# Two more chunks of ten get their layer-1 bias from GpSimd and ScalarE, not from a TensorE product

## The chip, the core and the metric

The kernel runs on one core of a Trainium2 chip. The time is device microseconds of one execution; 9 runs of the kernel before have a median of 577.31 us (576.45 to 579.66).

## What is computed

A graph layer over 128 graphs of 64 nodes with 128 channels. For each pair (i, j) of nodes in a graph a small network makes a message; the messages over the edges of the adjacency matrix are summed at i, and a second network of the same form updates the node:

```python
pair_feats = concatenate([f_i, f_j], axis=-1)            # 256 channels
h = layernorm(relu(pair_feats @ w0 + b0), g0, be0)       # layer 0
h = layernorm(relu(h @ w1 + b1), g1, be1)                # layer 1
messages = (h @ w2 + b2) * adj[..., None]
agg = messages.sum(axis=2)
out = x + mlp_upd(concatenate([x, agg], axis=-1))
```

All of it is float32.

## The kernel before

**Tiles and chunks.** The kernel computes messages for edges only. Two graphs make a pair; each graph of a pair has 640 edge places, which are filled by one-hot selection matrices (`S`, made of comparisons, with halves that are moved there by DMA). 128 edge places are a tile, four tiles a chunk (512 columns): 160 chunks in all. Five chunks are a quad (four graphs of edges), ten chunks a block (eight graphs, which share input loads and one update of 512 nodes).

**A chunk's path.** `layer0(n)` selects the two nodes' layer-0 rows with the S matrices (L539, TensorE) and ScalarE applies relu with the bias into `h` (L542). `stats0(n)` turns the four tiles (L548) and VectorE takes mean and variance of each edge (L552, `bn_stats`). The first layer norm is not applied to `h`: its scale is kept as one standard deviation per edge, and layer 1 is computed as relu(h w1c + std0 b1b), where `w1c` has the norm folded in. Since relu keeps a positive scale, the scale drops out in the second layer norm. `layer1(n)` computes h w1c into a PSUM bank `z` (L609, eight matmul records a chunk, two passes of each float32 product) and ScalarE applies the relu (L612) to give `y`; `stats1(n)` takes the statistics of `y` (L619). `reduce` sums `y` over the edges of each node, weighted by the inverse second deviation (L695).

**The bias std0 times b1b in the bank.** It is added in one of two ways:
- by TensorE: an extra product (L606) of the turned, split standard deviations `sdT` with a table `b1t`, 80 rows by 512 columns, ahead of the four products of the chunk;
- by a seed: ScalarE writes std0 times b1b into the bank beforehand (L597, four instructions of 128 columns, each scaled by one column of the standard deviations), and the products add to it.

From chunk 2 to chunk 151, those whose number ends in 0, 1, 2, 6, 7 or 9 are seeded, two iterations before their layer 1; all others have the TensorE product.

**The standard deviations.** Once per quad: when the fifth chunk's `stats0` is done, GpSimd computes m from the statistics (`square_sum`, L249 to L253), ScalarE takes the root m_sd (L259) and rounds it (`sh`, L566), GpSimd makes the rest of the split (L567), TensorE turns it (L572) and ScalarE copies it out (`sdT`, L577). A second such chain after layer 1 gives `m_sq` (L273, ScalarE) and its inverse `m_q` (L278, VectorE), from which GpSimd makes the weights `w` (L682).

**The order.** Nothing is scheduled automatically: `edge_path` records every engine's instructions in the order of the program. The main loop runs over iterations n; in each of them chunk n is in layer 0 and chunk n - 8 in layer 1 (`L1` = 8). Everything else is put into a plan by `at(n, place, function)`: it says in which iteration, and at which place in it, a function is called. The places come in the order a, m, [layer1], b, [layer0, stats0], k, [stats1], x, x1, x2, e0, e1, e. Each engine runs its instructions in that order, and waits where one needs something that is not there yet. In the timeline at 268 to 275 us iterations 79 to 82 are seen: the y at 268.24 is that of chunk 71, at 270.51 of chunk 72, at 272.63 of chunk 73.

**What else stands near the change.** In iterations that end in 9, 0 and 1: `distance` (d, L482, ScalarE), the update's `usdb` (L777, ScalarE), its turn `uh` (L740, TensorE), its copy `uhT` (L745, ScalarE) and its second layer (L754, TensorE), `residual` (xo, L734, GpSimd), `node_rows` (the cast i, L497, GpSimd). The layer-0 PSUM bank is a single one, so `layer0` of the next chunk waits for `h` of the one before; the layer-1 banks are two, used in turn.

**Inputs.** Blocks 0 and 1 have their adjacency and node features in buffers of their own (`an0`, `xn0`); those of later blocks rotate over three and five buffers and are loaded by SyncE's DMA queue, `load_adj` 25 iterations before the block. `odd_weights` checks that the adjacency is 0 or 1.

Of the kernel before, what the change touches and what calls it, by code (L numbers as in the profile page):

```python
# [9 lines left out]
F32 = mybir.dt.float32  # L10
# [4 lines left out]
ALU = mybir.AluOpType  # L15
# [8 lines left out]
def tile_gnn(  # L24
# [40 lines left out]
    nc = tc.nc  # L65
    B, N, C = x.shape
    P = 128
# [6 lines left out]
    CH = 4  # L74
    QC = QT // CH
    NCHK = NQ * QC
    PB = 4
    NB = NP // PB
    CPB = NCHK // NB

    xf = x.rearrange("b n c -> (b n) c")
    of = out.rearrange("b n c -> (b n) c")
    adjp = adj.rearrange("(p g) i j -> (g i) p j", g=2)

    const = ctx.enter_context(tc.tile_pool(name="const", bufs=1))
# [10 lines left out]
    def col(ap, name, eng=nc.sync):  # L96
        return load(ap.rearrange("(c o) -> c o", o=1), [P, 1], name, eng)
# [2 lines left out]
        return load(ap.rearrange("(o c) -> o c", o=1), [1, C], name, eng)  # L100


    an0 = const.tile([P, 2, PB, N], F32, name="an0")
    xn0 = const.tile([P, 2, PB, C], F32, name="xn0")

    def load_first(b, q0, q1):
        nc.sync.dma_start(xn0[:, b, q0:q1], xf[(b * PB + q0) * P:(b * PB + q1) * P, :]
                          .rearrange("(q p) c -> p q c", p=P))

    nc.sync.dma_start(an0[:, 0], adjp[:, 0:PB, :])  # L110
    load_first(0, 0, 2)
    w0a = mat(mw0[0:C, :], "w0a", nc.scalar)
    w0b = mat(mw0[C:2 * C, :], "w0b", nc.scalar)
    load_first(0, 2, PB)
    b0c = col(mb0, "b0c")
    nc.sync.dma_start(an0[:, 1], adjp[:, PB:2 * PB, :])
    load_first(1, 0, PB)
    w1 = mat(mw1, "w1")
    g0c = col(mg0, "g0c")
# [48 lines left out]
    W = {}  # L168
# [66 lines left out]
    def bc(t, n, axis=1):  # L235

        s = [P, n, C] if axis == 1 else [P, C, n]
        return t.unsqueeze(axis).to_broadcast(s)
# [48 lines left out]


    def edge_path(es):
        blkp = es.enter_context(tc.tile_pool(name="blk", bufs=3))  # L290
        adp = es.enter_context(tc.tile_pool(name="adp", bufs=2))
        tpp = es.enter_context(tc.tile_pool(name="tpp", bufs=8))
        sp = es.enter_context(tc.tile_pool(name="sp", bufs=4))
# [1 line left out]
        yp = es.enter_context(tc.tile_pool(name="yp", bufs=12))  # L295
        lp = es.enter_context(tc.tile_pool(name="lp", bufs=3))
        wp = es.enter_context(tc.tile_pool(name="wp", bufs=2))
        updp = es.enter_context(tc.tile_pool(name="upd", bufs=1))
        stp = es.enter_context(tc.tile_pool(name="stp", bufs=5))
        ps_k = es.enter_context(tc.tile_pool(name="ps_k", bufs=1, space=PSUM))  # L300
# [21 lines left out]
        def zbank(k):  # L322
            return ps_z[k].tile([P, CH * C], F32, name=f"z{k}")
# [4 lines left out]
        def at(n, place, fn, *args):  # L328
            plan.setdefault((n, place), []).append((fn, args))
# [3 lines left out]
                fn(*args)  # L333

        blocks = {b: {} for b in range(NB)}
        TP, S, H, ST0, V0, SD, SH, Y, ST1, Q, OH, WT, YS, MK, D, IR, JR, SR, Z = ({} for _ in range(19))


        def load_adj(b):
            if b < 2:  # L340
                blocks[b]["an"] = an0[:, b]
                return
            an = blkp.tile([P, PB, N], F32, name="an", bufs=3)
            nc.sync.dma_start(an, adjp[:, b * PB:(b + 1) * PB, :])
            blocks[b]["an"] = an

        def load_x(b):
            if b < 2:
                blocks[b]["xn"] = xn0[:, b]
                return  # L350
            xn = blkp.tile([P, PB, C], F32, name="xn", bufs=5)
            nc.sync.dma_start(xn, xf[b * PB * P:(b + 1) * PB * P, :]
                              .rearrange("(q p) c -> p q c", p=P))
            blocks[b]["xn"] = xn
# [225 lines left out]
        SEEDED = set()  # L580

        def z_of(n):

            if n not in Z:
                Z[n] = zbank(n % 2).rearrange("p (t c) -> p t c", t=CH)
            return Z[n]

        def seed(n):
# [6 lines left out]
            for t in range(CH):  # L595
                k = CH * c + t
                nc.scalar.activation(Z[n][:, t, :], W["b1b"], AF.Copy, scale=SR[q][:, k:k + 1])  # L597

        def layer1(n):

            q, c = divmod(n, QC)
            ps = z_of(n)
            del Z[n]
            h = H.pop(n)
            if n not in SEEDED:
                nc.tensor.matmul(ps, lhsT=SD[q], rhs=W["b1t"][:, CH * c:CH * c + CH, :],  # L606
                                 start=True, stop=False, skip_group_check=True)
            for t in range(CH):
                nc.tensor.matmul(ps[:, t, :], lhsT=h[:, t * P:(t + 1) * P], rhs=W["w1c"],  # L609
                                 start=False, stop=True, skip_group_check=True)  # L610
            Y[n] = yp.tile([P, CH, C], F32, name="y")
            nc.scalar.activation(Y[n], ps, AF.Relu)  # L612
# [190 lines left out]
        L1 = QC + 3  # L803
# [8 lines left out]
        for b in range(NB):  # L812
            o = b * CPB
            if b > 1:
                at(max(o - 25, 0), "a", load_adj, b)
                at(max(o - 12, 0), "a", load_x, b)
            if b > 0:
                r = max(o - 12, 1)
                at(max(o - 14, 0), "m", rank, b)
                at(r, "x", count, b)  # L820
                at(r + 1, "a", count_out, b)
                at(r + 1, "a", degrees, b)
                at(max(o - 9, r + 1), "e", place, b)
                at(max(o - 7, r + 3), "e", place_out, b)
                at(max(o - 7, 13), "m", odd_weights, b)
                at(o - 3, "x", turn_x, b)
                at(o - 2, "a", turn_x_out, b)
            for half, n in ((0, o - 2), (1, o + 3)):
                if n >= 0:
                    at(n, "x2", rows, b, half)  # L830
                    at(n + 1, "a", rows_hi, b, half)
                    at(n + 1, "m", rows_lo, b, half)
        for b in reversed(range(NB)):
            o = b * CPB
            n = o + QC + SC
# [35 lines left out]
        for p in range(NP):  # L871
            n = p * TG * 2 // CH
# [13 lines left out]
            q, h = divmod(p, 2)  # L886
# [4 lines left out]
        for q in range(NQ):  # L891
            n = q * QC + QC if q else LEAD
# [12 lines left out]
        for n in range(2, NCHK - L1):  # L905
            if n % CPB in (0, 1, 2, 6, 7, 9):
                at(n + L1 - 2, "x", seed, n)

        warm = ubank()
        for n in range(7):
            nc.tensor.matmul(warm[:, 0:P], lhsT=mean_m, rhs=mean_m, start=True, stop=True)
        load_adj(0)
        load_x(0)
        load_adj(1)
        load_x(1)
        rank(0)
        count(0)
# [54 lines left out]
        stats0(0)  # L974
        at(0, "x", turn_x, 0, 2, PB)
        at(1, "a", lambda: turn_x_out_rest())
        at(18, "m", odd_weights, 0)

        def turn_x_out_rest():
            nc.scalar.copy(blocks[0]["xnT"][:, 2 * P:PB * P], blocks[0].pop("x_ps")[:, 2 * P:])  # L980
# [46 lines left out]
        for n in range(last + 1):  # L1027
            run(n, "a")
            run(n, "m")
            if n == NCHK:  # L1030
                stats0(n - 1)
            if 0 <= n - L1 < NCHK:
                layer1(n - L1)
            run(n, "b")
            if n + LEAD < QC or QC <= n < NCHK:
                layer0(n if n >= QC else n + LEAD)
            if n + 1 < QC or QC <= n - 1 < NCHK - 1:
                stats0(n - 1 if n > QC else n + 1)
            run(n, "k")
            if 0 <= n - L1 < NCHK:  # L1040
                stats1(n - L1)
            for k in ("x", "x1", "x2", "e0", "e1", "e"):
                run(n, k)
# [3 lines left out]
    with ExitStack() as es:  # L1047
        es.enter_context(tc.manual_schedule())
        flag = edge_path(es)
# [160 lines left out]
```

## Time and profile before

| | |
|---|---|
| median of 9 runs | 577.31 us (576.45 to 579.66) |
| the profiled execution | 576.57 us, span 574.8 us |
| mean granted TensorE clock | 0.986 |
| ScalarE seeds L597 | 360, 133.6 us, 371 ns each |
| TensorE bias products L606 | 70, 33.8 us, 483 ns each |

Engines are PE (TensorE), PEld (its weight loads), DVE (VectorE), ACT (ScalarE), POOL (GpSimd) and SP (SyncE, which issues DMA). A line of the timeline gives the start in us from the start of the span, the length in us, the engine, the line of the kernel, the operation, what it writes and reads, and its size; in brackets stands the idle time of the engine before it and what ended it. Instructions of one engine overlap at their ends: the time that one costs is seen from its start to the next one's start.

### The profile page before, as it was taken

The numbers are of one execution on the slowest core, as the hardware profiler recorded it, in microseconds if no ns is written. First come the engines' busy times: TensorE is split into PE (matmuls) and PEld (weight loads), VectorE is DVE, ScalarE is ACT, GpSimd is POOL, SyncE is SP. The second block draws the span as 40 slices with busy tenths as digits, with TensorE's granted clock in tenths as the row PEclk, the third lists the DMA queues.
The fourth block names the chain that finished last, engine by engine and source line by source line (L and its number), as shares of the span: only waits on it lengthen the run. The fifth ranks groups of instructions, "written<-read, shape, count | busy, mean of one in ns | idle before, by whom it ended". The sixth has DMA issues, their size and how long they took to land. (4 is left out here: it accounts for less than half of the span.)

```text
span 574.8 us, 15748 instructions
## 1 busy us (share of the span) xinstructions
PE 548.9 (95%) x5303; PEld 514.9 (90%) x5303; DVE 479.8 (83%) x1944; ACT 476.7 (83%) x1149; POOL 339.4 (59%) x898
## 2 busy tenths in 40 slices
PE   6798999999999999999999999999999999998894
PEld 4597889999999999999999999999999999988883
DVE  5678789797989889798989989798988979896686
ACT  6677979898888989898888989888898989886434
POOL 3344465675757666565767657575766656556342
PEclk8889999999999999999999999999999999999999
DMA  4464535365564655458453554555465464631201
GB/s 101 102 146 107 127 93 143 93 118 127 125 135 107 140 108 130 106 108 153 113 141 83 140 114 116 127 125 134 99 136 120 121 106 99 135 93 31 35 21 40
DMA packets 90769, 63.21 MB, mean 110 GB/s; under 512 B 57398, under 2 KB 74812, under 8 KB 90684
## 3 DMA queue, kind: packets, MB, share of 16 engines
q1 hardware_dynamic: 90396, 62.03, 48.9%
q8 instruction: 43, 0.70, 0.5%
q14 instruction: 42, 0.34, 0.2%
q10 hardware_dynamic: 288, 0.13, 0.1%
HBM read 6.82 MB, written 4.19 MB: 19 GB/s over the span
## 5 line engine op out<-in xcount | busy, mean ns | idle before, releaser
L552 DVE BATCH_NORM_STATS2 st<-hT 128x6 f32<-128x128 f32 x640 | 142.2, 286 | 36.6 <-PE hT L548 35.2
L609 PE MATMUL z<-w1c,h 128*128 128x128 f32 x1280 | 172.2, 277 | 0.0
L609 PEld LDWEIGHTS z<-w1c,h 128*128 128x128 f32 x1280 | 161.1, 192 | 8.2 <-issue 5.1
L597 ACT ACTIVATE z<-b1b,m_sd 128x128 f32<-128x128 f32 x360 | 133.6, 371 | 8.7
L619 DVE BATCH_NORM_STATS2 st<-y 128x6 f32<-128x128 f32 x640 | 138.1, 281 | 2.7 <-ACT y L612 1.4
L612 ACT ACTIVATE y<-z 128x512 f32<-128x512 f32 x160 | 94.5, 591 | 26.6 <-PE z L609 24.9
L542 ACT ACTIVATE h<-hps,b0c 128x512 f32<-128x512 f32 x160 | 109.4, 684 | 4.0 <-PE hps L539 3.9
L548 PE MATMUL hT<-ident,h 128*128 128x128 f32 x640 | 98.2, 276 | 1.6 <-DVE st L552 1.5
L682 POOL TENSOR_TENSOR w<-oh,m_q 128x320 f32<-128x320 f16 x126 | 91.8, 741 | 9.9 <-PE hT L548 5.3
L539 PE MATMUL hps<-s,abl 128*128 128x512 f32 (+3 forms) x256 | 93.5, 377 | 1.7 <-DVE abl L473 0.9
L548 PEld LDWEIGHTS hT<-ident,h 128*128 128x128 f32 x640 | 76.9, 142 | 11.9 <-ACT h L542 1.3
L497 POOL CAST i<-tp 128x640 fp32r<-128x640 f16 x58 | 41.6, 718 | 66.6 <-DVE tp L488 48.7
L539 PE MATMUL hps<-s,abh 128*128 128x512 f32 (+3 forms) x256 | 79.7, 330 | 0.0
L695 PE MATMUL ys<-y,w 128*64 128x128 f32 x1280 | 76.9, 275 | 0.0
L695 PEld LDWEIGHTS ys<-y,w 128*64 128x64 f32 x1280 | 69.2, 137 | 4.2 <-issue 3.6
L249 POOL TENSOR_TENSOR m_d<-st 128x20 f32<-128x20 f32 x62 | 16.3, 263 | 91.0 <-DVE st L552 78.0
L521 DVE TENSOR_TENSOR j<-mk,cmpt 128x320 fp32r<-128x320 f32 x124 | 59.1, 476 | 3.0 <-PE mk L513 3.0
L539 PEld LDWEIGHTS hps<-s,abl 128*128 128x128 f32 x256 | 50.3, 196 | 3.6 <-ACT h L542 2.1
L482 ACT ACTIVATE d<-slot,mid 128x640 f16<-128x640 f16 x64 | 52.7, 824 | 0.0
L539 PEld LDWEIGHTS hps<-s,abh 128*128 128x128 f32 x256 | 50.5, 197 | 0.0
L473 DVE TENSOR_TENSOR abl<-mu,abh 128x512 fp32r<-128x512 f32 (+1 forms) x33 | 22.3, 675 | 31.2 <-ACT abh L467 31.1
L513 PE MATMUL mk<-tp,posall 128*128 128x320 f16 x126 | 38.2, 303 | 3.5 <-POOL posall L397 2.5
(224 smaller groups left out, 978.0 us busy)
## 6 DMA issues: line engine op xcount, KB each, us to landing
s<-i SPq DMA_DIRECT2D x124, 160.0 KB, 2.7
s<-j SPq DMA_DIRECT2D x124, 160.0 KB, 2.6
xn<-in_x_dram SPq DMA_DIRECT2D x15, 256.0 KB, 3.7
out_dram<-uo SPq DMA_DIRECT2D x15, 256.0 KB, 2.4
an<-in_adj_dram SPq DMA_DIRECT2D x16, 128.0 KB, 2.6
oh<-tp SPq DMA_TRANSPOSE x64, 3.4
xn<-in_x_dram SPq DMA_DIRECT2D x2, 128.0 KB
out_dram<-uo SPq DMA_DIRECT2D x2, 128.0 KB, 2.6
```

Source lines behind the costliest of these rows:

```text
L482: nc.scalar.activation(D[p], slot, AF.Abs, bias=blocks[b]["mid"][:, q:q + 1], scale=-1.0)
L521: nc.vector.tensor_tensor(JR[p][:, c], MK.pop((p, k))[:, 0:HC], cmpt[:, c], op=ALU.is_equal)
L539: nc.tensor.matmul(ps[:, c:c + w], lhsT=ab[:, g % 4, :], rhs=s, start=(k == 0), stop=(k == 1))
L542: nc.scalar.activation(H[n], ps, AF.Relu, bias=b0c)
L548: nc.tensor.transpose(ps[:, t, :], H[n][:, t * P:(t + 1) * P], ident)
L552: nc.vector.bn_stats(ST0[q][:, CH * c + t, :], ps[:, t, :])
L597: nc.scalar.activation(Z[n][:, t, :], W["b1b"], AF.Copy, scale=SR[q][:, k:k + 1])
L609: nc.tensor.matmul(ps[:, t, :], lhsT=h[:, t * P:(t + 1) * P], rhs=W["w1c"], start=False, stop=True, skip_group_check=True)
L612: nc.scalar.activation(Y[n], ps, AF.Relu)
L619: nc.vector.bn_stats(ST1[q][:, CH * c + t, :], Y[n][:, t, :])
L682: (nc.vector if p == NP - 2 else nc.gpsimd).tensor_tensor(WT[p][:, :, g, :], OH[p][:, :, g * N:(g + 1) * N], Q[q][:, k:k + TG].unsqueeze(2 ...
L695: nc.tensor.matmul(YS[b][g * N:(g + 1) * N, k, :], lhsT=w[:, t, g, :], rhs=y, start=(t == 0), stop=(t == TG - 1))
```

## The change

Chunks whose number ends in 3 or 4, from chunk 3 to 144, are no longer biased by TensorE: these are 30 chunks. In iteration n + 5 of chunk n, at its last place, GpSimd multiplies b1b by the chunk's four standard deviations, 128 by 512, into a new tile `sb` (two buffers). In iteration n + 6, place x, ScalarE copies it into the bank. The 30 L606 go; chunks that end in 5 or 8 keep theirs, so that the turn of the standard deviations stays.

The buffers of blocks 0 and 1 become the first of the rotating ones, so the separate 6 KB per partition go. For that `load_adj` comes 19 and not 25 iterations before its block, and `odd_weights` of block 0 is called in iteration 9 and not 18. In the built program the DVE order differs only in that last step; SyncE has its loads in the new places; no other instruction changes its place.

```diff
-    an0 = const.tile([P, 2, PB, N], F32, name="an0")
-    xn0 = const.tile([P, 2, PB, C], F32, name="xn0")
+    blkp = ctx.enter_context(tc.tile_pool(name="blk", bufs=3))
+    an0 = [blkp.tile([P, PB, N], F32, name="an", bufs=3) for b in range(2)]
+    xn0 = [blkp.tile([P, PB, C], F32, name="xn", bufs=5) for b in range(2)]
...
+        sbp = es.enter_context(tc.tile_pool(name="sbp", bufs=2))
...
+        def products(n):
+
+            q, c = divmod(n, QC)
+            SB[n] = sbp.tile([P, CH, C], F32, name="sb")
+            nc.gpsimd.tensor_tensor(SB[n], bc(W["b1b"], CH), SR[q][:, CH * c:CH * c + CH]
+                                    .unsqueeze(2).to_broadcast([P, CH, C]), op=ALU.mult)
+
+        def seed_from(n):
+            z_of(n)
+            SEEDED.add(n)
+            nc.scalar.copy(Z[n], SB.pop(n))
...
-                at(max(o - 25, 0), "a", load_adj, b)
+                at(max(o - 19, 0), "a", load_adj, b)
...
             if n % CPB in (0, 1, 2, 6, 7, 9):
                 at(n + L1 - 2, "x", seed, n)
+            elif n % CPB in (3, 4):
+                at(n + L1 - 3, "e", products, n)
+                at(n + L1 - 2, "x", seed_from, n)
...
-        at(18, "m", odd_weights, 0)
+        at(9, "m", odd_weights, 0)
```

More of the change, by code (lines that the diff above doesn't have):

```diff
@@ L100, in row @@
         return load(ap.rearrange("(o c) -> o c", o=1), [1, C], name, eng)
-    an0 = const.tile([P, 2, PB, N], F32, name="an0")
-    xn0 = const.tile([P, 2, PB, C], F32, name="xn0")
+    blkp = ctx.enter_context(tc.tile_pool(name="blk", bufs=3))
+    an0 = [blkp.tile([P, PB, N], F32, name="an", bufs=3) for b in range(2)]
+    xn0 = [blkp.tile([P, PB, C], F32, name="xn", bufs=5) for b in range(2)]
     def load_first(b, q0, q1):
-        nc.sync.dma_start(xn0[:, b, q0:q1], xf[(b * PB + q0) * P:(b * PB + q1) * P, :]
+        nc.sync.dma_start(xn0[b][:, q0:q1], xf[(b * PB + q0) * P:(b * PB + q1) * P, :]
                           .rearrange("(q p) c -> p q c", p=P))
-    nc.sync.dma_start(an0[:, 0], adjp[:, 0:PB, :])
+    nc.sync.dma_start(an0[0], adjp[:, 0:PB, :])
     load_first(0, 0, 2)
@@ L115, in tile_gnn @@
     b0c = col(mb0, "b0c")
-    nc.sync.dma_start(an0[:, 1], adjp[:, PB:2 * PB, :])
+    nc.sync.dma_start(an0[1], adjp[:, PB:2 * PB, :])
     load_first(1, 0, PB)
@@ L289, in edge_path @@
     def edge_path(es):
-        blkp = es.enter_context(tc.tile_pool(name="blk", bufs=3))
         adp = es.enter_context(tc.tile_pool(name="adp", bufs=2))
@@ L335, in edge_path @@
         blocks = {b: {} for b in range(NB)}
-        TP, S, H, ST0, V0, SD, SH, Y, ST1, Q, OH, WT, YS, MK, D, IR, JR, SR, Z = ({} for _ in range(19))
+        TP, S, H, ST0, V0, SD, SH, Y, ST1, Q, OH, WT, YS, MK, D, IR, JR, SR, Z, SB = ({} for _ in range(20))
         def load_adj(b):
             if b < 2:
-                blocks[b]["an"] = an0[:, b]
+                blocks[b]["an"] = an0[b]
                 return
@@ L348, in load_x @@
             if b < 2:
-                blocks[b]["xn"] = xn0[:, b]
+                blocks[b]["xn"] = xn0[b]
                 return
```

## The prediction

> **What bounds the kernel now.** I read the page's totals first, then the busy time of one stretch of the steady part, then the timeline of each engine inside it.
>
> ```profile
> PE 548.9 (95%) x5303; PEld 514.9 (90%) x5303; DVE 479.8 (83%) x1944; ACT 476.7 (83%) x1149; POOL 339.4 (59%) x898
> ```
> ```profile
> 263.00:296.00 33.00, 33.00 (x332) 31.55 (x331) 29.11 (x120) 29.48 (x72) 21.31 (x57) 1.00 0.59 122
> ```
> The second line (us, then PE, PEld, DVE, ACT, POOL busy, granted clock) says that TensorE has no idle time there. The first y relu (L612) of a block stands at 263.44 and that of the next block at 296.28: 32.85 us for ten chunks, within 0.03 in all blocks from 100 to 490 us. So a matmul that goes is time won, unless TensorE then has to wait. Whether it has to is seen at the place of the two removed matmuls, where the ScalarE queue runs like this (start, length, what; in brackets idle time before):
>
> ```profile
> 269.59 0.83 ACT L482 ACTIVATE d<-slot,mid 128x640 f16<-128x640 f16 x1
> 270.31 0.30 ACT L273 ACTIVATE m_sq<-m_v,eps_c 128x20 f32<-128x20 f32 x1
> 270.51 0.59 ACT L612 ACTIVATE y<-z 128x512 f32<-128x512 f32 x1
> 270.99 0.69 ACT L542 ACTIVATE h<-hps,b0c 128x512 f32<-128x512 f32 x1
> 271.56 0.41 ACT L777 ACTIVATE usdb<-bu1b,um_sd 128x128 f32<-128x128 f32 x1
> 271.85 0.59 ACT L745 COPY uhT<-ma 128x512 f32<-128x512 f32 x1
> 272.63 0.60 ACT L612 ACTIVATE y<-z 128x512 f32<-128x512 f32 x1 [0.19 <-PE z L609]
> 273.40 0.31 ACT L259 ACTIVATE m_sd<-m,eps_c 128x20 f32<-128x20 f32 x1 [0.17 <-POOL m L253]
> 273.75 0.22 ACT L566 CAST sh<-m_sd 128x40 fp32r<-128x40 f32 x1
> ```
> ScalarE has 83% over the span, but here it runs from 268.24 to 273.40 with 0.36 us of rest, all of it after 272.44. On TensorE and its weight loads:
>
> ```profile
> 270.87 0.60 PE L740 MATMUL ma<-ident,uh 128*128 128x128 f32 x4
> 271.23 0.47 PE L606 MATMUL z<-b1t,sdT 80*128 80x512 f32 x1
> 271.54 1.05 PE L609 MATMUL z<-w1c,h 128*128 128x128 f32 x8
> 274.51 0.48 PE L606 MATMUL z<-b1t,sdT 80*128 80x512 f32 x1
> 274.82 0.27 PE L609 MATMUL z<-w1c,h 128*128 128x128 f32 x1
> ```
> ```profile
> 274.37 0.12 PEld L572 LDWEIGHTS ma<-ident,sh 128*80 128x80 f32 x1
> ```
> Between the two removed L606 stands L572, the turn of the split standard deviations. It needs sh from GpSimd:
>
> ```profile
> 272.97 0.40 POOL L253 TENSOR_TENSOR m<-m_d,m_s 128x20 f32<-128x20 f32 x1
> 274.05 0.27 POOL L567 TENSOR_TENSOR sh<-m_sd,sh 128x40 fp32r<-128x40 f32 x1
> ```
> sh ends at 274.32 and L572's weights start at 274.37. Where TensorE demonstrably waits for sh, they start 0.05 us after its end too:
>
> ```profile
> PEld ma L572 <- POOL sh L567: 4.0, 3, 1.5
> ```
> So this chain (statistics of chunk 79 on VectorE, five GpSimd steps, root m_sd and split on ScalarE, sh on GpSimd, L572) has no slack at all, though no idle time shows it. It is the point on which the change turns.
>
> **The change part by part.** *Removed: 30 L606.* A row says 0.47 us, but matmuls overlap, so the price is what it adds between its neighbours. L740 to L609 takes 0.67 us with L606 (270.87 to 271.54) and 0.44 without (284.21 to 284.65); L572 to L609 takes 0.34 with (274.48 to 274.82) and 0.11 without (291.07 to 291.18). That is 0.23 us each, 6.9 us in all if nothing waits.
>
> *Added: 30 GpSimd products* (512 columns, two inputs). The nearest rows are xo L734, 1.28 us, and the bias table L659 on 80 partitions, 1.13 us. Two per block stand around xo at 264.03; with them GpSimd is done by about 267.7. Its next step starts at 268.83 after 3.53 us of idle time, so the products hide in that gap, and ScalarE needs the first at 269.6. Queued behind them are xo (nine iterations before its use), the cast i (which waits for VectorE until 268.83 anyway) and nothing else. If that cover were gone, each us late would be a us of ScalarE wait per block. The Trainium skill (GPSIMD Engine Reference, Engine selection) speaks against this step: a two-input elementwise operation is about twice as slow there as on VectorE. By that rule the step is badly placed; by the idle row it costs nothing, and the sum uses the row.
>
> *Added: 30 ScalarE copies* of 512 columns from SBUF to PSUM, which the trace does not have. What counts is the time c from its start to the next instruction's. Lower bound: the same copy from PSUM, L745 or L612, 0.48. Upper bound: the cast of 640 columns from SBUF, L495, 0.63 (31.73 to 32.37). Columns cost 0.84 ns (d L482 at 0.72 for 640 against usdb L777 at 0.29 for 128), so 128 columns off the cast leave c = 0.52, which I take. The Trainium skill (ScalarE: Activation LUTs, Step-by-step) says that writing PSUM is faster than writing SBUF; the seeds L597 are indeed shorter than usdb (371 against 396 ns), but their start-to-next is 0.31 against 0.29, so I give no discount. With 25 ns off, the sum below would come out 0.4 to 0.6 us lower.
>
> *Where the copies stand.* By the built order the first stands between usdb and d (269.59), the second between usdb and uhT (271.85). What is queued behind them moves:
> 1. The first moves m_sq by c. VectorE's L278 waits for m_sq (it starts 0.03 after it, as at 286.39) and had 0.07 us to spare at 270.72; so it and the statistics behind it move by c - 0.07 = 0.45, and m on GpSimd and m_sd with them.
> 2. Both move uhT, y and m_sd in ScalarE's own order: y then starts at 272.33 + 2c, m_sd at 272.81 + 2c, that is 2c - 0.59 = 0.45 later than before.
> 3. By either way sh and L572 are 0.45 us late: weights at 274.82. After such a wait the next matmul follows 0.145 us later (62.30 to 62.45 behind L572), so L609 starts at 274.96, where before it started at 274.82, 0.45 behind the same weights: **0.14 us later**, where the two removed matmuls alone would have made it 0.46 earlier. On the way TensorE also waits about 0.15 for h (end 272.20) at the next L539; that wait lies inside the later one.
> 4. After that ScalarE has a rest of 0.63 us before the next y, so the lateness is TensorE's alone and the next block starts with the old phase.
>
> The tight place occurs in 13 blocks (L572 at 110, 143, ... 504 us): 13 x 0.14 = +1.8 us. In the first two blocks TensorE already waits over 1 us at L572 (45.89, 78.44), so the first removed matmul gains nothing; the second gains 0.23 in each, less 0.16 in the second block, where m_sq had 0.36 to spare before VectorE asks for it: -0.3 us. Sum: **+1.5 us** on the profiled execution, 576.57 to 578.1. That execution lies 0.74 below the median, so the predicted median is 577.31 + 1.5 = 578.8.
>
> *Moved at no cost.* The sharing of buffers issues the same loads. The adjacency load goes six iterations later, ahead of the s<-i transfers: its issue of 0.59 us falls into SyncE's wait for the cast i (277.37), it lands 2.6 us later and is read five iterations (16 us) later; if late, rank and the statistics behind it would wait. odd_weights(0) goes from iteration 18 to 9: two VectorE steps of 0.41 and 0.42 us in a stretch where VectorE has 26.4 us of 33; from -0.8 to +0.8 us if that cover fails, and I take 0.
>
> **The rivals.**
> *Faster: the chain does not move.* The mechanism: TensorE keeps what it saves. For it speaks that TensorE is full and ScalarE only 89% busy in the stretch. If the copies cost the chain nothing, L572 still waits for sh at 274.37 and only the second removal counts: 15 x 0.23 to 0.31 = -3.5 to -4.7, 572.6 to 573.8; if the chain came earlier too, -6.9, 570.4. The point of decision is c: below 0.38, where c - 0.07 is less than the 0.45 - 0.145 = 0.31 that L606's absence saves behind L572, the block gets shorter. Against it: 128 columns alone take 0.31.
> *Slower by more: c is at its upper bound.* With c = 0.63 the queue moves m_sd by 0.67, a block loses 0.36, 13 x 0.36 - 0.3 = +4.4, 581.7.
> *GpSimd late:* products behind a wait for statistics. 2 us of margin at 269.6 speak against it; each us beyond is +13, so 590 and up.
> *No net change:* gain and loss meet, as at c = 0.48 (0.41 - 0.31 = +0.10 per block, +1.0, 578.3); that is the lower end of my own forecast.
>
> **How the numbers follow.** A measurement here tells 0.2%, 1.2 us, from no change. My forecast has 0.68, and its own range is c from 0.48 to 0.60: 578.3 to 580.9; about two fifths of it lie within 0.2%. The faster rival has 0.15, the dear copy 0.13, late GpSimd 0.04. So faster 0.15, same 0.27, slower 0.58. The range reaches below the forecast to half of the smaller gain and above to the dear copy: 577.31 - 1.7 = 575.6, and 581.7.
>
> **What would show it.** Right: L572 waits, its weights 0.05 us after sh in every block, m_sd without idle time before it or 0.45 later after the block's start, L278 waiting for m_sq, and a block of 33.0 us. Wrong: a block near 32.4 us with TensorE full, a copy whose start-to-next is below 0.4, or ScalarE waiting for sb.

## The result, and the profile after

The changed kernel takes 580.44 us (median of 10 runs, 579.57 to 582.44) beside 577.59 us for the kernel before on the same chip (31 runs): a ratio of 1.0058 with a 95% interval of 1.0045 to 1.0071. That is slower by 2.6 to 4.1 us, where 1.5 us were forecast. (The two medians lie 2.85 us apart; the means of the same runs, 581.02 and 577.66 us, have the ratio 1.0058.) The profiled execution took 580.34 us with a span of 578.6 us.

30 matmuls and 30 x 0.23 us of TensorE work are gone, and the kernel is slower. The change moved every line of the file: L572 is now L573 (turn of `sh`), L278 is L279 (`m_q`), L606 is L619 (bias product), L609 is L622 (products of layer 1), L612 is L625 (`y`); `uhT` is now L758, the matmuls behind it L767; the new products are L604, the new copies L610.

The busy time of the same stretch of 33 us (us, then PE, PEld, DVE, ACT, POOL busy, granted clock):

```profile
263.00:296.00 33.00, 32.86 (x329) 31.02 (x327) 28.95 (x119) 30.24 (x74) 23.09 (x59) 1.00 0.56 120
```

On the page 5273 matmuls are recorded where there were 5303, but TensorE's busy sum is not smaller (550.7 us, before 548.9), and in the stretch it now has 0.14 us without work where it had none. The waits say for whom (who waits, for whom; us in total, times, longest). Two lines of the changed kernel, and below them the second of the two before:

```profile
PEld ma L573 <- POOL sh L568: 8.6, 16, 1.5
DVE m_q L279 <- ACT m_sq L274: 10.2, 28, 0.7
```
```profile
DVE m_q L278 <- ACT m_sq L273: 5.2, 15, 0.7
```

Before, L572 waited for sh 3 times, 4.0 us in all; now it waits 16 times. The 13 new ones, 0.33 us each, stand once in every later block (4.3 us; the first of the three old ones has also grown, by 0.24). VectorE's L278 waited for m_sq 15 times; 13 more waits have come, 0.38 us each.

The groups of the new instructions (us in all, mean ns of one; idle time before them in us):

```profile
L604 POOL TENSOR_TENSOR sb<-b1b,m_sd 128x512 f32<-128x512 f32 x30 | 31.1, 1039 | 0.0
L610 ACT COPY z<-sb 128x512 f32<-128x512 f32 x30 | 18.0, 602 | 0.0
```

Neither has idle time before it: ScalarE never waits for `sb`, so GpSimd is in time. GpSimd's idle time ahead of the cast i, in which the prediction put the products, has gone from 3.53 to 1.53 us. The times of a block are measured below from the y of its second chunk (chunk 71 here), which stands ahead of the first copy. That y before:

```profile
268.24 0.60 ACT L612 ACTIVATE y<-z 128x512 f32<-128x512 f32 x1
```

and ScalarE's timeline in the changed kernel, from the same y through the tight place:

```profile
270.59 0.61 ACT L625 ACTIVATE y<-z 128x512 f32<-128x512 f32 x1
...
271.95 0.60 ACT L610 COPY z<-sb 128x512 f32<-128x512 f32 x1
272.46 0.84 ACT L483 ACTIVATE d<-slot,mid 128x640 f16<-128x640 f16 x1
273.19 0.31 ACT L274 ACTIVATE m_sq<-m_v,eps_c 128x20 f32<-128x20 f32 x1
...
274.74 0.60 ACT L610 COPY z<-sb 128x512 f32<-128x512 f32 x1
275.26 0.60 ACT L758 COPY uhT<-ma 128x512 f32<-128x512 f32 x1
275.74 0.62 ACT L625 ACTIVATE y<-z 128x512 f32<-128x512 f32 x1
276.22 0.33 ACT L260 ACTIVATE m_sd<-m,eps_c 128x20 f32<-128x20 f32 x1
276.58 0.23 ACT L567 CAST sh<-m_sd 128x40 fp32r<-128x40 f32 x1
```

The two brackets with idle time that stood before y and before m_sd are gone: the queue is now full up to the cast. VectorE's step behind m_sq, before and in the changed kernel, and then what follows on GpSimd, TensorE's weight loads and TensorE:

```profile
270.72 0.26 DVE L278 RECIPROCAL m_q<-m_sq 128x20 f32<-128x20 f32 x1
```
```profile
273.53 0.28 DVE L279 RECIPROCAL m_q<-m_sq 128x20 f32<-128x20 f32 x1 [0.38 <-ACT m_sq L274]
```
```profile
275.69 0.40 POOL L254 TENSOR_TENSOR m<-m_d,m_s 128x20 f32<-128x20 f32 x1
...
276.89 0.27 POOL L568 TENSOR_TENSOR sh<-m_sd,sh 128x40 fp32r<-128x40 f32 x1
```
```profile
277.21 0.12 PEld L573 LDWEIGHTS ma<-ident,sh 128*80 128x80 f32 x1 [0.33 <-POOL sh L568]
```
```profile
277.35 1.06 PE L622 MATMUL z<-w1c,h 128*128 128x128 f32 x8
```

Measured from the y of chunk 71, sh's weights come at 6.62 us (277.21 - 270.59) and came at 6.13 (274.37 - 268.24): 0.49 later. The next L622 comes at 6.76 and came at 6.58: 0.18 later. That is all of a block's loss: 33.03 us where it was 32.85.

### The profile page after: what moved, and what is told of

The parts are those of the page before. It is cut to its first block, busy times and chain, and to the rows that moved or that the text cites. A ratio compares the mean times of both kernels' runs of the same rounds, so it can differ in the third digit from the quotient of the medians.

```text
span 578.6 us, 15793 instructions
## 1 busy us (share of the span) xinstructions
PE 550.7 (95%) x5273; PEld 510.4 (88%) x5273; DVE 481.3 (83%) x1944; ACT 491.0 (85%) x1179; POOL 368.4 (64%) x928
## 5 line engine op out<-in xcount | busy, mean ns | idle before, releaser
L622 PE MATMUL z<-w1c,h 128*128 128x128 f32 x1280 | 172.3, 277 | 0.0
L622 PEld LDWEIGHTS z<-w1c,h 128*128 128x128 f32 x1280 | 159.1, 192 | 7.2 <-issue 5.1
L625 ACT ACTIVATE y<-z 128x512 f32<-128x512 f32 x160 | 94.9, 594 | 17.7 <-PE z L622 16.0
```

## The experiments

Each was timed in five rounds beside the kernel before, which had a median of 577.35 us beside e1 to e4 and 577.12 beside e5 to e8. "Block" is the time from the y of one block's second chunk (71, 81 and so on) to the next one's, in the steady part; "that y" is always the one of chunk 71. Two theories stood against each other: that the copies' *places* in ScalarE's queue delay the chain to L573; and that the change *loads* something (GpSimd's products, more ScalarE work, the loads moved). The runs also separate the two copies.

**e1_buffers: the moved loads alone.** Shared buffers, `load_adj` and `odd_weights` as changed, without the new way of the bias:

```diff
-            elif n % CPB in (3, 4):
-                at(n + L1 - 3, "e", products, n)
-                at(n + L1 - 2, "x", seed_from, n)
```

> The changed kernel with its shared buffers, its later adjacency loads and its earlier odd_weights, but chunks 3 and 4 of ten biased by TensorE as before. Theory (ScalarE's order delays the chain to L572): no product, no copy, so no change, block 32.85 us and 577.6 us (576.8 to 578.4). Rival (the moved loads or the moved odd_weights cost the part of the loss that the blocks do not show, seen before the first y): +0.6 to +1.6, 578.2 to 579.2.

Measured: 577.57 us, ratio 1.0004 (0.9989 to 1.0020), block 32.85. The loads and `odd_weights` in their new places cost nothing that this interval (0.2% at most) can show.

**e2_only4: the second copy alone**, the one between usdb and uhT.

```diff
-            elif n % CPB in (3, 4):
+            elif n % CPB in (4,):
```

> The changed kernel, but only chunk 4 of ten gets the GpSimd product and the ScalarE copy; chunk 3 has its TensorE product. Theory: with one copy behind the y of chunk 2, m_sq is not delayed and m_sd stays within ScalarE's 0.36 us of rest (0.52 - 0.59 is below 0), so L572 keeps its time and the L606 behind it is saved: a block is 0.31 us shorter, 32.54, and the whole about -0.31 x 13 - 0.3 = -4.3, 573.3 us. Rival (each product and copy costs by its load on ScalarE or GpSimd, wherever it stands): half of the loss of the whole change, +1.4, 579.0 us.

Measured: 574.19 us, ratio 0.9939 (0.9920 to 0.9958): faster than the kernel before. Block 32.63, 0.22 less. The waits of this kernel show the two numbers that the kernel before had, and its ScalarE and weight-load timelines the reason (that y at 267.76):

```profile
DVE m_q L279 <- ACT m_sq L274: 5.2, 15, 0.7
...
PEld ma L573 <- POOL sh L568: 4.0, 3, 1.5
```
```profile
271.38 0.61 ACT L610 COPY z<-sb 128x512 f32<-128x512 f32 x1
...
272.92 0.31 ACT L260 ACTIVATE m_sd<-m,eps_c 128x20 f32<-128x20 f32 x1
```
```profile
273.89 0.12 PEld L573 LDWEIGHTS ma<-ident,sh 128*80 128x80 f32 x1
```

m_sd comes 5.16 us after that y and the weights 6.13, both as before. The copy went into rests that ScalarE had behind uhT: from uhT to m_sd it is 1.03 us from start to start (uhT at 271.89), before 1.55, and m_sd had been waiting for GpSimd's m in any case. So the chain stays and TensorE keeps the matmul that it no longer does. The saving is the plain 0.23, not the 0.31 expected: the expectation took the 0.145 us from weights to products that belongs to a waiting TensorE, but here TensorE comes to the turn no earlier than sh does, its L573 matmul starts at 6.24 as before, and L622 follows at 6.35 where it was 6.58.

**e3_only3: the first copy alone**, the one ahead of d and m_sq.

```diff
-            elif n % CPB in (3, 4):
+            elif n % CPB in (3,):
```

> The changed kernel, but only chunk 3 of ten gets the GpSimd product and the ScalarE copy; chunk 4 has its TensorE product. Theory: m_sq and with it VectorE's L278 and the statistics behind it are 0.45 us late, L572 too, and L606 behind it stays: a block is some 0.38 us longer, 33.23, and the whole +0.38 x 13 = +4.9, 582.5 us, more than with both. Rival (cost by load): half of the loss of the whole change, +1.4, 579.0 us.

Measured: 583.48 us, ratio 1.0094 (1.0072 to 1.0116). With *half* of the added work a block is longer than with the whole change: 33.12 us, 0.27 more than before. Its waits, and the ScalarE and weight-load timelines (that y at 271.38):

```profile
PEld ma L573 <- POOL sh L568: 8.9, 16, 1.5
```
```profile
276.90 0.31 ACT L260 ACTIVATE m_sd<-m,eps_c 128x20 f32<-128x20 f32 x1 [0.29 <-POOL m L254]
```
```profile
277.86 0.12 PEld L573 LDWEIGHTS ma<-ident,sh 128*80 128x80 f32 x1 [0.36 <-POOL sh L568]
```

Here ScalarE stands idle ahead of m_sd, waiting for m: the delay came by way of m_sq, VectorE's L279 and the statistics behind it. m_sd is at 5.52 us (0.36 later than before) and the weights at 6.48 (0.35 later). So this way alone gives 0.35, not the 0.45 of my first step. L622 follows those weights by 0.38 (0.45 before), which leaves the 0.27 of the block. 13 x 0.27 = 3.5 us.

Besides, one block late in the profiled execution (from the y of chunk 140 to that of chunk 150) took 35.3 us and not 33.4; in e7 and e8 it took 34.7 and 35.2. The granted TensorE clock goes with it. The pages give it in tenths for 40 equal slices of the span; the changed kernel's line, and e3's:

```profile
PEclk9989999999999999999999999999999999999999
```
```profile
PEclk9989999999999999999999999999999999998999
```

In e3 the clock is 0.5 for 3.4 us from 525.1 us on, in e7 from 516.4, in e8 from 521.8; none of the other seven profiles has this late stretch. 3.4 us at half clock are 1.7 us less of work at the full one, an estimate that fits the 1.6 us by which these blocks exceed those of a kernel with the same steady block (e8 that of the changed kernel, 33.55 us; e7 that of e4, 33.09). So some 1.6 of e3's 583.48 us come with the clock and not with its order: its one run with a granted clock of 0.994 took 581.94 us. That is 4.6 above the kernel before at such a clock (577.3, below), where 3.5 in the blocks and 0.7 at the start add up to 4.2. Three timed runs of the changed kernel with a clock of 0.991 likewise took 582.4 us, where seven with 0.995 took 580.2 to 580.5. What set the clock back isn't shown.

**e4_dearly: both copies, but `distance` out of the way.** The whole change, with the d that stands between the first copy and m_sq moved to two iterations earlier:

```diff
-                    at(max(n - 7, p - 2), "a", distance, p)
+                    if p % 4 == 3 and p > 4:
+                        at(n - 9, "x", distance, p)
+                    else:
+                        at(max(n - 7, p - 2), "a", distance, p)
```

> The whole change, and the one d per block that stands between the first copy and m_sq (0.72 us on ScalarE) is made two iterations earlier, where ScalarE waits 1.08 us for TensorE. Theory: m_sq comes before VectorE asks for it and m_sd is free by ScalarE's order, so sh and L572 are as early as before the change, TensorE waits there by the saved 0.23 us and keeps the other saving: block 32.54 us, 573.3 us. Rival (the two copies or products cost by load, not by place): as the changed kernel, 33.03 us a block, 580.4 us.

Measured: 574.90 us, ratio 0.9956 (0.9936 to 0.9976), block 32.53. All 30 copies and products are there, no instruction less on any engine, and the kernel is 5.5 us faster than the changed one. The ScalarE timeline shows the copy now straight ahead of m_sq, which ends before VectorE needs it; the weights follow that y (268.46) by 6.13 again:

```profile
269.81 0.60 ACT L610 COPY z<-sb 128x512 f32<-128x512 f32 x1
270.33 0.31 ACT L274 ACTIVATE m_sq<-m_v,eps_c 128x20 f32<-128x20 f32 x1
```
```profile
274.59 0.12 PEld L573 LDWEIGHTS ma<-ident,sh 128*80 128x80 f32 x1
```

The block's gain of 0.32 is the 0.46 that both matmuls gave up, less the 0.14 by which TensorE now waits for a chain that has not moved. In the first block the early d cost 0.6 us (e5, the same move without the change, lost 0.45 there), and the first y came late as in the changed kernel (37.46 us), so the total fell short of what was expected.

**e5_before_dearly: the same move of d in the kernel before.**

> The kernel before, with the one d per block that stands ahead of m_sq made two iterations earlier, and nothing else. Theory: TensorE is full in every block, so a chain to L572 that comes earlier gains nothing: block 32.85 us, 577.4 us (576.6 to 578.2). Rival (it is the early d by itself that made the fourth kernel faster): block 32.54 us, 573.4 us.

Measured: 577.68 us, ratio 1.0013 (1.0004 to 1.0022), block 32.85. The move by itself gains nothing (the 0.1% that it loses is about the 0.45 us of its first block), so what e4 gains it gains from the change.

**e6_dearly_mq: the chain made earlier too.** As e4, with `inverse_of` (m_sq and m_q) from place m to place k, and the first product behind the last b1t:

```diff
-            at(end + wait, "m", inverse_of, q)
+            at(end + wait, "m" if last or q == NQ - 2 else "k", inverse_of, q)
...
-                at(n + L1 - 3, "e", products, n)
+                at(*((9, "a") if n == 3 else (n + L1 - 3, "e")), products, n)
```

> The whole change with three moves: the early d; the inverse m_q on VectorE behind the statistics of layer 0 and not ahead of them (0.22 us of the chain to L572); and the first product of chunk 3 behind the last piece of the bias table on GpSimd. Theory: the chain reaches L572 at or before TensorE, so all of the 0.46 us are kept: block 32.39 us, -0.46 x 13 - 0.3 = -6.3, 571.1 us. Rival (TensorE waits at another place, for h or uhT): block 32.54, as in the fourth kernel, 574.0 us.

Measured: 573.98 us, ratio 0.9951 (0.9936 to 0.9967), block 32.43 to 32.46. The steady block gained 0.40 of the 0.46 us: the weights now come 6.04 us after that y (6.13 in e4), still 0.05 behind the end of sh. The whole gained less than the theory says: 0.5 us went behind the y of chunk 150, some 0.5 in the first block, and the first y came at 37.28 us (in a profile with half the granted clock for 6.8 us from 28.3 on, where that of before has it for 3.4). It beats both kernels, but by no more than e2 does.

**e7_nocopy: the products without the copies.** GpSimd's 30 products run; chunks ending in 3 and 4 get no bias at all:

```diff
-            nc.scalar.copy(Z[n], SB.pop(n))
+            SB.pop(n)
...
-                                  start=False, stop=True, skip_group_check=True)
+                                  start=n in SEEDED and n % CPB in (3, 4), stop=True, skip_group_check=True)
```

> The whole change without the ScalarE copies: GpSimd makes its products, nobody reads them, and the four products of these chunks overwrite the bank, so that chunks 3 and 4 of ten lack the bias. Theory (the copies' place in ScalarE's order is the cost): L572's chain is as early as before, TensorE waits there by the saved 0.23 and a block is 0.31 us shorter, 32.54; -0.31 x 13 - 0.3 + 0.7 at the start = -3.6, 573.8 us. Rival (GpSimd's 31 us of products slow VectorE or ScalarE): as the changed kernel, 33.03 us, 580.4 us.

Measured: 573.59 us, ratio 0.9940 (0.9925 to 0.9954), block 32.54. That is e4's block, in which the copies were there: in the steady blocks the 30 products of 1.04 us cost nothing, and neither do the copies once d doesn't stand behind the first of them, ahead of m_sq.

**e8_late3: the start.** The whole change, with only chunk 3's product put behind the last piece of the table b1t:

```diff
-                at(n + L1 - 3, "e", products, n)
+                at(*((9, "a") if n == 3 else (n + L1 - 3, "e")), products, n)
```

> The whole change with the first product of chunk 3 behind the last piece of the bias table on GpSimd, and not between the fourth and the fifth. In the four profiles with that product in its place a scan of VectorE at 31 us took 1.7 to 1.85 us, in the profiles without it 0.85. Theory: that order belongs to the 1 us before the first y, so the scan takes 0.85 again and the whole is 0.6 to 1.0 us shorter, 579.5 us, at the same 33.03 us a block. Rival (the scan's length is chance and the start has nothing to do with the order): 580.4 us.

Measured: 579.75 us, ratio 1.0050 (1.0036 to 1.0064), block 33.00 to 33.03. VectorE's scan at 30.7 us, which took 1.85 us in the changed kernel, takes 0.85 as it did before, and the first y comes at 37.0 and not 37.7 us. The median is 0.7 us below that of the whole change, but the kernels before beside them differ by 0.5 and the two intervals of the ratio overlap: the scan is shown, its price in the time is only likely.

## Why the prediction was right, and where its sizes were off

The direction, the mechanism and the range held. Step by step:

- **TensorE has no idle time, and the chain to L572 no slack: right.** The weights start 0.05 us after sh in the tight place of every block (e.g. 277.16 to 277.21), as announced; block 33.03 us where 33.0 was announced. m_sd has no idle time before it and L279 waits for m_sq. The Trainium skill (Perfetto Trace Analysis, Identifying the Most-Contended Engine) says to optimize first the engine with the highest occupancy, and to judge TensorE's headroom by its MFU or the busy share of its weight loads. TensorE is that engine by either busy share (matmuls 95%, weight loads 90%; VectorE and ScalarE 83%), and the change took work off it; e3 took 15 matmuls off it and its block got 0.27 us longer. In this case the rule holds only as long as what the engine waits for has slack.
- **c, the copy's price: right.** 516 to 519 ns from its start to the next start in all 30 places, taken as 0.52 us; the discount for writing PSUM, which I refused, does not show. (That discount was also worth less than I wrote: 25 ns off c move the later of the two ways by 25 ns, and 13 x 0.025 = 0.3 us, not 0.4 to 0.6.) The rival of the dear copy (0.63) and the faster rival's condition (c below 0.38) both fall with that.
- **Step 1, by way of m_sq: mechanism right, size off.** L279 moves by 0.46 as expected (2.94 us after the y of chunk 71, before 2.48), but m on GpSimd only by 0.37 (5.10 against 4.73): the bn_stats group right behind L279 takes 0.82 us now and took 0.89, and it starts 0.19 us behind L279's start where it was 0.22. e3 shows this way alone: 0.35 for the expected 0.45.
- **Step 2, by ScalarE's own order: this one decides.** m_sd moves by 0.47 (5.63 against 5.16; expected 0.45), and starts 0.13 after m has ended, where behind a real wait it starts 0.03 after. So with both copies ScalarE's queue is the later way, by about 0.1; with the first copy alone it is m's (e3); with the second alone there is no delay at all (e2). I had the two ways as equal.
- **Step 3: term mis-sized.** 0.49 us at the weights (expected 0.45) and L622 0.14 behind them (expected 0.145). A block loses 0.18, not 0.14, and 13 x 0.18 = +2.3 us where the sum had +1.8. On the way TensorE's weight loads also wait 13 times, some 0.2 us each, for uhT (L767), which the step didn't name; by its order, like the wait for h that it did name, this lies inside the later one.
- **First two blocks: mis-sized.** From the first y of the run to that of chunk 20 they gain 0.05 and 0.14, together 0.2 where the sum had 0.3.
- **The start: not in the sum.** From the first y to that of chunk 150 the profiled executions differ by 2.2 us, the terms above together. The other 1.6 of their 3.8 us lie *before* the first y (36.07 and 37.72 us). The sum had costed the products in the steady block alone, where a gap of GpSimd hides them, and taken that for all 30. The first stands among the pieces of b1t, a stretch where GpSimd has no gap. With it there the first y came at 37.46 to 37.72 us (the change, e3, e4), without it at 36.97 and 37.04 (e8, e2): 0.4 to 0.75 us less, 0.75 between the change and e8. These five profiles have the granted clock in common: full until 0.5 for 3.4 us from about 30 us on.
- **The other 0.9 us of the 1.6 is not the change's.** The profile before has a clock of 0.5 from 8.8 to 19.0 us as well, where that of the changed kernel has the full one. Up to the end of b1t, e1 and e2 run the same instructions, the moved loads among them; e1, with half the clock from 11.8 to 18.6 us, came to its first y at 35.49 us, e2, without, at 37.04. Why the executions with the early half clock come there sooner isn't shown. The timed runs agree: of the kernel before, beside the experiments, those with a mean clock of 0.985 or 0.986 (as its profile) took 576.2 to 576.8 us, those with 0.994 or 0.995 took 577.0 to 577.9, median 577.3; the changed kernel with 0.995 (as its profile) took 580.2 to 580.5. At the same clock that is 3.0 us, beside the 2.2 + 0.7 = 2.9 us of the terms.
- **GpSimd late, and no net change:** the first falls with the copies' idle time of 0.0; for the second, the ratio's interval excludes 1.
- **The moved loads at 0: right**, as far as e1's interval can tell.
- **0.23 us for each removed matmul: right**, as e2's block shows (0.22).

So this is where the 6.9 us of TensorE's work went. In each of 13 blocks the two matmuls gave up 0.46 us. Had the chain stayed where it was, TensorE would have waited 0.14 of them for it and kept 0.32 (e4). The copies set the chain 0.49 us later, and 0.32 - 0.49 is the loss of 0.17 to 0.18.

## What to carry to other kernels

Work taken from a full engine is a gain only where what the engine waits for comes early enough: look for the producer that ends just ahead of its consumer (here 0.05 us, with no idle time in the profile), and count how much later the change makes it. In an engine that runs in order, the place of an added instruction can count for more than its length; here, with the copy behind m_sq, a block took 0.22 us less, with the same copy ahead of d and m_sq 0.27 us more, and moving that one d from between them was worth 5.5 us in all. Compare profiled executions at the same granted clock: 0.9 of the 3.8 us between the two profiles came with the clock. Price an added instruction also in the first blocks, where the gap that hides it in the steady part may not be there yet.

## What the runs showed of the hardware that I had not expected

**A scan on VectorE ended only behind a piece of GpSimd's work.** The rank scan has two inputs in SBUF and takes 0.67 to 0.71 us in 15 of its 16 places. At about 30 us it stands beside GpSimd's five b1t products. The VectorE timelines of the changed kernel and, below it, of e8:

```profile
30.77 1.85 DVE L360 TENSOR_TENSOR_SCAN rk<-first,an 128x256 f32<-128x256 f32 x1
```
```profile
30.73 0.85 DVE L360 TENSOR_TENSOR_SCAN rk<-first,an 128x256 f32<-128x256 f32 x1
```

and in the GpSimd timeline of the changed kernel the product stands ahead of the fifth piece:

```profile
30.04 4.50 POOL L672 TENSOR_TENSOR b1t<-b1mix,tile_of 80x512 fp32r<-80x512 f32 x4
34.50 1.04 POOL L604 TENSOR_TENSOR sb<-b1b,m_sd 128x512 f32<-128x512 f32 x1
35.49 1.04 POOL L672 TENSOR_TENSOR b1t<-b1mix,tile_of 80x512 fp32r<-80x512 f32 x1
```

It took 1.71 to 1.85 us in all four kernels with that order (the change, e3, e4, e7) and 0.72 to 0.85 in the six without. In all ten traces it ends 0.55 us after the end of a b1t piece: of the first piece in the six, of the second, 1.04 us on, in the four. The piece that runs beside the scan's end takes 1.42 us where most take 1.04, and the cast tp next to it on VectorE, 0.37 to 0.40 us in nearly all other places, takes 1.1 in all ten. The Trainium skill (Perfetto Trace Analysis, Optimizing Scalar/DVE Operations) says that GpSimd and VectorE share an SBUF read port, which some VectorE operations hold alone; these rows agree with that. Why the scan lets one piece more go first when the product stands *four microseconds later* in GpSimd's queue isn't shown by any run.

**A two-input product on GpSimd with both inputs broadcast took 1.04 us** for 128 by 512, less than the rows that I had taken as the nearest (1.13 and 1.28 us). The 1.13 was a mean of five pieces of b1t, of which three took 1.04 and the two beside the scan and the cast 1.42 and 1.11.
